# Stage 1 of a fused triangle layer: normalisation shifts stored as 16-byte pieces from tokens on partitions

## The chip, the core and the metric

The kernel runs on one core of a Trainium2 chip. Its five engines run their own instruction lists and meet at semaphores: TensorE (PE in the profile; PEld is its weight load), VectorE (DVE), ScalarE (ACT), GpSimd (POOL) and SyncE (SP), which here issues nearly all DMAs. The metric is device time in microseconds (us) for one execution, as the median of several. All data are float32.

## What is computed

Two layers over x of shape 384 x 384 x 128 (positions i and k, 128 channels). The first is a triangle layer, the second a gated row layer:

```
z     = layernorm(x)                                   # over the channels
left  = (z @ Wl + bl) * sigmoid(z @ Wlg + blg)
right = (z @ Wr + br) * sigmoid(z @ Wrg + brg)
core  = einsum('ikh,jkh->ijh', left, right)
x1    = x + sigmoid(x @ Wg + bg) * (layernorm(core) @ Wout + bout)

left2 = x1 @ W_left + b_left + x1 @ W_eq + b_eq
rsum  = sum over k of (x1 @ W_right + b_right)
y     = (left2 * rsum * sigmoid(x1 @ W_gate + b_gate)) @ W_out + b_out
out   = layernorm(y + x1)
```

The change is in the making of `left` and `right` alone.

## The kernel before

The kernel has three stages. Stage 1 makes `left` and `right` for all tokens and stores them to DRAM (`lr_d`). Stage 2 multiplies them channel by channel (L608). Stage 3 does everything that follows, row by row. Only stage 1 is touched.

Stage 1 works in 144 chunks. A chunk is 8 positions i times 128 positions k. It is done in two steps of four i each, so there are 288 steps. The code of a loop over `steps` is written out as one list for each engine, in program order. The order of the calls in that loop is the order of work on each queue.

The layer norm is split. Its weight is folded into the matrix `wz` (128 x 512), and its two numbers per token are used at different places:

- The scale `rs`, one over the standard deviation, is applied after the matmul, when PSUM is read out (L383 on ACT, L385 on DVE).
- The shift, a value per token that is subtracted from all channels, has to be applied to x before the matmul (L318 or L322 on GpSimd).

To get both, DVE runs `bn_stats` on tokens (L264, in `stats`), turns the results of a batch of chunks into means and variances (L276 to L280, in `powers`), GpSimd raises the variance to the power -1/2, one chunk at a time (L287, in `power`), and DVE makes the shift from it (L297 to L300, in `centres`). `LEAD` says how many steps the statistics run ahead of the steps that use them; `goal` gives their pace. Batches have one, two or four chunks.

The first 8 chunks are "plain". For them x lies with tokens on partitions, GpSimd subtracts the shift there (L318), and TensorE turns the result so that channels lie on partitions (L333). All other chunks load x a second time with channels on partitions (`columns`, L135). Their shift has to lie along the free dimension, in one row that is then broadcast over the partitions. `store_nd` does this: TensorE turns a batch's shifts (L348), ACT copies them out and halves them (L350), and SP stores them to the DRAM tensor `nd_d` (L351). Six steps before a step needs them, `load_shift` loads one row of 512 numbers (2 KB) back (L140). In `shift`, GpSimd broadcasts that row to all partitions (L321) and subtracts it from the columns (L322), two steps ahead of the matmuls.

In `back`, four matmuls with 512 output columns (L373) use 128 columns of x each as their weights.

GpSimd's instructions come from libraries that can be loaded. The loop asks for one twice (L470):

```
if k > 0:
    more = 4 if k in (6, len(steps) - 6) else 1
    while shifted < min(len(steps), k + 2 + more):
        shift(*steps[shifted])
        shifted += 1
    if more > 1:
        lib = library_config.all_libraries[10] if k == 6 else library_config.standard
        seq(nc.gpsimd.load_library(lib))
```

At step 6 it is the library with index 10, six steps before the end it is the standard one. In both places the subtractions of four steps are issued ahead of the load.

SP's queue is in order as well. It holds, for each step, a store of shifts if one is due, the columns of a chunk four ahead, one or more shift rows, a chunk of tokens, and a slice of `lr` (1 MB) to store. A DMA that has to wait holds back those behind it.

Of the kernel before, what the change touches and what calls it, by code (L numbers as in the profile page):

```python
# [8 lines left out]
F32 = mybir.dt.float32  # L9
AF = mybir.ActivationFunctionType  # L10
ALU = mybir.AluOpType
# [3 lines left out]
P = 128  # L15
# [4 lines left out]
def triangle_then_gated_row_kernel(ctx: ExitStack, tc: tile.TileContext, a: dict, out: bass.AP):  # L20
# [13 lines left out]
    nc = tc.nc  # L34
    x_nat, x_tok, x_row = a["x_nat"], a["x_tok"], a["x_row"]
    NG8, C = x_nat.shape[1], x_tok.shape[2]
    N = 8 * NG8
# [18 lines left out]
    def seq(ins):  # L56

        return tc.keep_in_program_order(ins)
# [21 lines left out]
    with ExitStack() as ctx2:  # L80
# [16 lines left out]
        with tc.tile_pool(name="p1w", bufs=5, side="right") as wp, \  # L97
# [1 line left out]
             tc.tile_pool(name="p1c", bufs=4, side="right") as xcp, \  # L99
             tc.tile_pool(name="p1n", bufs=4, side="right") as bcp, \  # L100
             tc.tile_pool(name="p1s", bufs=14, side="right") as sp, \
             tc.tile_pool(name="p1d", bufs=2, side="right") as dp, \
             tc.tile_pool(name="p1t", bufs=2, space=PSUM) as tps, \
             tc.tile_pool(name="p1p", bufs=3, space=PSUM) as pps:
            NQ = XR // 4
            AHEAD, LEAD = 4, 25
            TURN, FETCH = 9, 6
            HS = H // 8
            loaded, normed = {}, {}
            lr, full = {}, []  # L110
            batches, at = [(n, n + 1) for n in range(PLAIN)], PLAIN
            for size in [1, 1] + [2] * 7 + [4] * len(chunks):
                if at < len(chunks):
                    batches.append((at, min(at + size, len(chunks))))
                    at = batches[-1][1]
# [14 lines left out]
            def load_columns(n):  # L130

                if PLAIN <= n < len(chunks):
                    columns[n] = xcp.tile([P, XR, P], F32, tag="xt", name="xc")
                    src = x_tok[n // NG8, n % NG8]
                    seq(nc.sync.dma_start(out=columns[n].rearrange("c i k -> c (i k)"), in_=src))  # L135

            def load_shift(n, q):

# [84 lines left out]
            def late_weights():  # L223

                m2 = bcp.tile([P, 4 * P], F32, tag="bc", name="m2")[:, :C]
                seq(nc.vector.tensor_scalar(m2, avg, go, -0.5, ALU.mult, ALU.mult))

                seq(nc.vector.tensor_add(wleft, wleft, weq))
                seq(nc.vector.tensor_add(bleft, bleft, beq))

                seq(nc.vector.tensor_scalar(lns, lns, -1.0, None, ALU.mult))
                return m2
# [15 lines left out]
            def stats(n, q, half):  # L252

                if q == 0 and half == 0:
                    own = batch[n]
                    if n == own[0]:
                        g = XR * (own[1] - own[0])
                        terms[own] = [sp.tile([P, 4 * XR, 6], F32, tag="st", name="st", bufs=2)[:, :g]]
                    normed[n] = own, XR * (n - own[0])
                own, c0 = normed[n]  # L260
                st = terms[own][0][:, c0:c0 + XR]
                r0 = 4 * q + 2 * half
                for r in range(r0, r0 + 2):
                    seq(nc.vector.bn_stats(st[:, r, :], loaded[n][:, r, :]))  # L264

            def powers(own, lo, hi):

                if lo == 0:
                    g = XR * (own[1] - own[0])
                    terms[own] += [sp.tile(s, F32, tag=t, name=t, bufs=c)[:, :g] for t, s, c in  # L270
                                   ((f"mv{g}", [P, g, 2], {XR: 3, 2 * XR: 2}.get(g, 1)),
                                    ("nd", [P, 4 * XR], 3) if own[0] >= PLAIN else ("nd0", [P, XR], PLAIN),
                                    ("rs", [P, 4 * XR], 7) if own[0] >= PLAIN else ("rs0", [P, XR], PLAIN))]
                st, mv, sd, rs = (t[:, lo:hi] for t in terms[own])
                dv = st[:, :, 1]
                seq(nc.vector.tensor_add(mv, st[:, :, 1:3], st[:, :, 4:6]))  # L276
                seq(nc.vector.tensor_sub(dv, dv, st[:, :, 4]))
                seq(nc.vector.tensor_scalar(sd, mv[:, :, 1], 4.0 / C, 4.0 * EPS, ALU.mult, ALU.add))
                seq(nc.vector.tensor_mul(dv, dv, dv))
                seq(nc.vector.tensor_add(sd, sd, dv))  # L280
                pows.extend((own, c, min(c + XR, hi), (lo, hi)) for c in range(lo, hi, XR))

            def power():

                own, lo, hi, span = pows.pop(0)
                sd, rs = (t[:, lo:hi] for t in terms[own][2:])
                seq(nc.gpsimd.tensor_tensor(rs, sd, mhalf[:, :hi - lo], ALU.pow))  # L287
                if hi == span[1]:
                    means.append((own, span))

            def centres(count):

                for _ in range(count):
                    own, (lo, hi) = means.pop(0)
                    _, mv, nd, rs = (t[:, lo:hi] for t in terms[own])
                    nds[own] = terms[own][2]
                    seq(nc.vector.tensor_mul(nd, nd, rs))  # L297
                    seq(nc.vector.tensor_sub(nd, mv[:, :, 0], nd))
                    if own[0] < PLAIN:
                        seq(nc.vector.tensor_scalar(nd, nd, 0.5, None, ALU.mult))  # L300
                    centred[own] = now[0]

            centred, now = {}, [-1]

            def free(own):
                flying = {p[0] for p in pows} | {p[0] for p in means}
                size = own[1] - own[0]
                return sum(o[1] - o[0] == size for o in flying) < {1: 3, 2: 2}.get(size, 1)

            means = []  # L310

            def shift(n, q, rows=slice(0, 4)):


                s = slice(4 * q + rows.start, 4 * q + rows.stop)
                if n < PLAIN:
                    nd = nds[n, n + 1][:, s].unsqueeze(2).to_broadcast([P, rows.stop - rows.start, C])
                    seq(nc.gpsimd.tensor_tensor(loaded[n][:, s], loaded[n][:, s], nd, ALU.subtract))  # L318
                else:
                    z, t = columns[n][:, s].rearrange("c i k -> c (i k)"), shifts.pop((n, q))  # L320
                    seq(nc.gpsimd.partition_broadcast(t, t[0:1]))  # L321
                    seq(nc.gpsimd.tensor_tensor(z, z, t, ALU.subtract))  # L322

# [19 lines left out]

            def store_nd(own):

                g = XR * (own[1] - own[0])
                pt = tps.tile([P, 4, P], F32, tag="pt", name="pt")
                seq(nc.tensor.transpose(pt[:g, 0], nds.pop(own), ident))  # L348
                ndt = dp.tile([4 * XR, P], F32, tag="ndt", name="ndt", bufs=1)
                seq(nc.scalar.activation(ndt[:g], pt[:g, 0], AF.Copy, scale=0.5))  # L350
                seq(nc.sync.dma_start(  # L351
                    out=nd_d[own[0]:own[1]].rearrange("n (i k) -> (n i) k", k=P), in_=ndt[:g]
                ))

            def store_slice():
# [8 lines left out]
            def back(n, q, half, between=None):  # L364
# [5 lines left out]
                t = lr[kb, ig]  # L370
                pr = pps.tile([P, 2, 4 * H], F32, tag="pr", name="pr")
                for r in range(2):
                    seq(nc.tensor.matmul(  # L373
                        pr[:, r, :], lhsT=columns[n][:, 4 * q + 2 * half + r, :], rhs=wz, start=True, stop=True
                    ))
                    if r == 0 and between:
                        between()
# [56 lines left out]
                    power()  # L434
            shifted = 2
            waiting = batches[AHEAD // NQ:]
            turning = batches[PLAIN:]

            def goal(k):

                return 2 * (k + 1 + min(LEAD, 5 + min(k, 12 + (k - 12) // 3))) if k >= 0 else 2 * AHEAD

            for n in range(PLAIN, len(chunks)):
                k = 2 + (n - PLAIN) // 2
# [3 lines left out]

            def begin(k):

                while waiting and 2 * NQ * waiting[0][1] <= given and free(waiting[0]):
                    own = waiting.pop(0)
                    powers(own, 0, XR * (own[1] - own[0]))
                    if k > 0:
                        break

            for k, (n, q) in enumerate(steps):
                now[0] = k
                early = len(means)
                for _ in range(min(len(pows), 1)):  # L460
                    power()
# [28 lines left out]
                    power()  # L490
                if q == NQ - 1:
                    del loaded[n], normed[n], columns[n]
                while turning and turning[0] in centred and (
                        k >= centred[turning[0]] + 2 or NQ * turning[0][0] - 6 <= k):
                    store_nd(turning.pop(0))
                if q == NQ - 1:
                    load_columns(n + 4)
                for m, mq in steps[k + FETCH:k + FETCH + 1]:
                    if m >= PLAIN:
                        load_shift(m, mq)  # L500
                for m in fetch.get(k, []):
                    load_chunk(m)
                store_slice()
# [2 lines left out]
                        load(t, src)  # L506
                if k == 20:
                    m2 = late_weights()
                if k == 21:
                    late_products(m2)  # L510
                if k == len(steps) - 2 * G // 4 + 16:
                    assert not full
# [466 lines left out]
```

## Time and profile before

| | |
|---|---|
| median of 3 runs | 3164.53 us (3163.78 to 3166.14) |
| the profiled execution | 3163.46 us, span 3161.7 us |
| TensorE's clock | 0.999 of full |
| TensorE busy | 3141.8 us (99%) |
| DVE, GpSimd, ACT busy | 2454.2, 2396.7, 1811.4 us |
| last matmul of stage 1 (L373) ends | 1017.7 us |
| DMA queue of SP, share of 16 engines | 73.0% |

The span is the time from the first to the last instruction in the record. A group's row gives line, engine, operation, output and inputs with their shapes and the count; then the total busy time, the mean in ns of one, and the idle time of the engine just ahead of such instructions, with what ended it. In a timeline, a row begins with start and duration in us. In the chain of work that ended last, each piece is what the end of the kernel depended on at that moment.

### The profile page before, as it was taken

The page shows a single profiled execution, that of the slowest core. Times are in us where ns is not written, and L with a number is a line of the kernel's source. Part 1 is how long each engine was busy: PE and PEld are TensorE (multiplying, and loading weights), DVE is VectorE, ACT ScalarE, POOL GpSimd, SP SyncE. Part 2 cuts the span into 40 slices and gives each one's busy share as a digit, 9 for nine tenths or more (in the row PEclk, how much of TensorE's full clock was granted, in tenths as well). Part 3 has the DMA queues.
Part 4 walks back from the last instruction along what each step waited for, and adds up shares of the span by engine and source line. Part 5 has one row for each costly group of instructions (what it writes and reads, how often), then busy time and mean ns, then how long its engine had stood idle before and what let it go on. Part 6 is the DMA issues. An engine that isn't in the chain of part 4 may idle for free.

```text
span 3161.7 us, 44412 instructions
## 1 busy us (share of the span) xinstructions
PE 3141.8 (99%) x11345; PEld 1873.7 (59%) x11345; DVE 2454.2 (78%) x7208; ACT 1811.4 (57%) x3794; POOL 2396.7 (76%) x3045
## 2 busy tenths in 40 slices
PE   9999999999999999999999999999999999999998
PEld 4444444444444666666666666677777777777776
DVE  8888888788875555555555788888888888888998
ACT  4444444444444333343343577677777777777777
POOL 5888888888885666666666587788888888888887
PEclk9999999999999999999999999999999999999999
DMA  4887878788773999999999865666666666666562
GB/s 170 329 320 293 333 271 331 282 320 307 296 291 91 284 280 284 281 285 282 282 283 284 295 237 199 223 223 220 220 220 220 220 220 220 220 220 220 210 211 110
DMA packets 474845, 797.41 MB, mean 252 GB/s; under 512 B 21345, under 2 KB 385313, under 8 KB 458210
## 3 DMA queue, kind: packets, MB, share of 16 engines
q1 hardware_dynamic: 473296, 792.61, 73.0%
q8 instruction: 94, 1.54, 0.2%
q10 hardware_dynamic: 1234, 1.77, 0.2%
q14 instruction: 157, 1.29, 0.1%
q0 software_dynamic: 64, 0.20, 0.0%
HBM read 508.14 MB, written 286.36 MB: 251 GB/s over the span
## 4 chain that ended last, share of the span: by engine, by line
PE 97%; DVE 1%; POOL 1%; ACT 0%; issue 0%; DMA 0%; POOLq 0%; DVEq 0%; ACTq 0%
PE pr L373 30%; PE pc L608 23%; PE py L778 8%; PE pr L749 8%; PE pg L766 8%; PE pl L767 8%; PE pg L718 8%; PE py L779 4%; POOL rs L287 0%; DVE st L264 0%; DVE lr L385 0%; PE pq L726 0%; POOL stage L318 0%; PE pt L348 0%; PE pt L333 0%
## 5 line engine op out<-in xcount | busy, mean ns | idle before, releaser
L373 PE MATMUL pr<-wz,xc 128*128 128x512 f32 x2176 | 939.2, 592 | 0.0
L383 ACT ACTIVATE sg<-pr,rs 128x256 f32<-128x256 f32 x1152 | 482.9, 470 | 511.9 <-ACT sg L383 322.8
L608 PE MATMUL pc<-rr,lrh 128*128 128x384 f32 x2304 | 743.3, 486 | 0.4 <-DVE lr L385 0.4
L373 PEld LDWEIGHTS pr<-wz,xc 128*128 128x128 f32 x2176 | 408.0, 190 | 518.1 <-issue 440.9
L385 DVE SCALAR_TENSOR_TENSOR lr<-pr,rs,sg 128x256 f32<-128x256 f32 x1152 | 501.4, 476 | 195.1 <-ACT sg L383 194.5
L608 PEld LDWEIGHTS pc<-rr,lrh 128*128 128x128 f32 x2304 | 452.0, 196 | 291.9 <-issue 1.2
L813 ACT ACTIVATE py<-py,nm,rs 128x128 f32<-128x128 f32 x1149 | 492.1, 429 | 160.8 <-DVE u L771 79.0
L778 PEld LDWEIGHTS py<-wo,u 128*128 128x128 f32 x2304 | 376.6, 191 | 97.5
L619 DVE TENSOR_TENSOR csum<-csum,ct 128x1152 f32<-128x1152 f32 x127 | 176.6, 1391 | 329.0 <-ACT ct L617 329.0
L778 PE MATMUL py<-wo,u 128*128 128x128 f32 x2304 | 402.1, 275 | 0.0
L617 ACT COPY ct<-pc 128x1152 f32<-128x1152 f32 x127 | 142.2, 1119 | 445.2 <-PE pc L608 439.6
L740 POOL TENSOR_TENSOR cs<-ct,rt 128x384 f32<-128x384 f32 x380 | 379.6, 1000 | 7.6 <-PE pr L749 4.3
L848 POOL TENSOR_TENSOR yt<-yt,lnb 128x384 f32<-128x384 f32 x380 | 380.3, 1002 | 2.9 <-DVE yt L842 2.9
L322 POOL TENSOR_TENSOR xc<-xc,bc 128x512 f32<-128x512 f32 x272 | 345.4, 1270 | 24.0
L287 POOL TENSOR_TENSOR rs<-nd,mhalf 128x8 f32<-128x8 f32 (+1 forms) x145 | 236.2, 1629 | 153.0 <-DVE nd L280 145.5
L793 DVE BATCH_NORM_STATS2 st<-py 128x6 f32<-128x128 f32 x1152 | 266.0, 286 | 86.6 <-PE py L779 84.6
L779 PE MATMUL py<-ident,x1T 128*128 128x128 f32 x1152 | 314.0, 273 | 0.0
L749 PE MATMUL pr<-cs,wc 128*128 128x384 f32 x768 | 313.5, 490 | 0.0
L766 PE MATMUL pg<-x1T,mat_L_conv_W_gate 128*128 128x384 f32 x768 | 310.7, 486 | 0.9 <-ACT g L769 0.9
L718 PE MATMUL pg<-xt,mat_L_conv_Wg 128*128 128x384 f32 x768 | 310.7, 487 | 0.3 <-ACT ct L632 0.2
L767 PE MATMUL pl<-x1T,mat_L_conv_W_left 128*128 128x384 f32 x768 | 310.5, 486 | 0.0
L589 POOL COPY rr<-lrh 128x768 f32<-128x768 f32 x128 | 194.6, 1520 | 152.9 <-DMA lrh<-lr_d 141.9
(125 smaller groups left out, 4299.2 us busy)
## 6 DMA issues: line engine op xcount, KB each, us to landing
lr_d<-lr SPq DMA_DIRECT2D x128, 1024.0 KB
lrh<-lr_d SPq DMA_DIRECT2D x128, 640.0 KB
xt<-in_x_row_dram SPq DMA_DIRECT2D x96, 768.0 KB
ct<-core_d SPq DMA_DIRECT2D x95, 768.0 KB
rt<-rstd_d SPq DMA_DIRECT2D x95, 768.0 KB
out_dram<-yt SPq DMA_DIRECT2D x94, 768.0 KB
core_d<-ct SPq DMA_DIRECT2D x125, 576.0 KB
xt<-in_x_nat_dram SPq DMA_DIRECT2D x136, 512.0 KB
```

Source lines behind the costliest of these rows:

```text
L373: seq(nc.tensor.matmul(pr[:, r, :], lhsT=columns[n][:, 4 * q + 2 * half + r, :], rhs=wz, start=True, stop=True))
L383: seq(nc.scalar.activation(sg[r], pr[:, r, 2 * H:], AF.Sigmoid, scale=rs[r]))
L385: seq(nc.vector.scalar_tensor_tensor(t[:, :, c * XR + r0 + r, :], pr[:, r, :2 * H].rearrange("k (h s) -> k h s", s=2), rs[r], sg[r].rearra ...
L608: seq(nc.tensor.matmul(banks[ib], lhsT=t[:, kb, ib * P:(ib + 1) * P, 0], rhs=rr[:, kb], start=(kb == 0), stop=(kb == NB - 1),))
L718: seq(nc.tensor.matmul(pg[:, :N], lhsT=wg0, rhs=r["xT"], start=True, stop=True))
L749: seq(nc.tensor.matmul(pr[:, :N], lhsT=wc, rhs=r["cs"], start=True, stop=True))
L766: seq(nc.tensor.matmul(pg2[:, :N], lhsT=wgate, rhs=r["x1T"], start=True, stop=True))
L767: seq(nc.tensor.matmul(pl[:, :N], lhsT=wleft, rhs=r["x1T"], start=True, stop=True))
L778: seq(nc.tensor.matmul(py[:, s], lhsT=r["u"][:, s], rhs=r["wo"], start=True, stop=False))
L779: seq(nc.tensor.matmul(py[:, s], lhsT=r["x1T"][:, s], rhs=ident, start=False, stop=True, is_transpose=True))
L813: seq(nc.scalar.activation(py[:, s], py[:, s], AF.Identity, bias=bias, scale=scale))
L848: seq(engine.tensor_tensor(yt, yt, lnbb, ALU.add))
```

## The change

The shifts of the chunks that are not plain are no longer turned on TensorE. SP stores them from where they lie, with tokens on partitions: each partition holds, for each group of four i, four numbers in a row, and these 16 bytes go to DRAM as one piece. The row that is loaded back then has its numbers in the order (k, i) instead of (i, k). The host lays out x's columns (`x_tok`) in the same order, so a weight load for one i now takes every fourth number.

With it come these edits:

- Batches have two chunks at most; `LEAD` is 15 instead of 25, with another `goal`.
- `centres` takes two fused operations on DVE, which halve the shift as well. For plain chunks 1 to 7 it takes three operations on GpSimd, called directly behind the power.
- `store_nd` is called in the step in which the shift was made. A row is loaded six steps ahead, or later where its store is younger than two steps, and at the latest three steps ahead.
- `late_weights` gets a tile of its own, and `late_products` moves from step 21 to step 24.

The diff, cut to its core:

```diff
-            AHEAD, LEAD = 4, 25
-            TURN, FETCH = 9, 6
+            AHEAD, LEAD = 4, 15
+            FETCH = 6
...
-            for size in [1, 1] + [2] * 7 + [4] * len(chunks):
+            for size in [1, 1] + [2] * len(chunks):
...
-                    columns[n] = xcp.tile([P, XR, P], F32, tag="xt", name="xc")
+                    columns[n] = xcp.tile([P, NQ, P, 4], F32, tag="xt", name="xc")
...
-                m2 = bcp.tile([P, 4 * P], F32, tag="bc", name="m2")[:, :C]
+                m2 = wp.tile([P, C], F32, tag="m2", name="m2", bufs=1)
...
                 if hi == span[1]:
                     means.append((own, span))
+                    if 0 < own[0] < PLAIN:
+                        centres(1)
...
                     nds[own] = terms[own][2]
-                    seq(nc.vector.tensor_mul(nd, nd, rs))
-                    seq(nc.vector.tensor_sub(nd, mv[:, :, 0], nd))
-                    if own[0] < PLAIN:
-                        seq(nc.vector.tensor_scalar(nd, nd, 0.5, None, ALU.mult))
-                    centred[own] = now[0]
...
+                    if 0 < own[0] < PLAIN:
+                        seq(nc.gpsimd.tensor_tensor(nd, nd, rs, ALU.mult))
+                        seq(nc.gpsimd.tensor_tensor(nd, mv[:, :, 0], nd, ALU.subtract))
+                        seq(nc.gpsimd.tensor_scalar(nd, nd, 0.5, 0.0, ALU.mult, ALU.add))
+                    else:
+                        seq(nc.vector.scalar_tensor_tensor(nd, nd, 0.5, rs, ALU.mult, ALU.mult))
+                        seq(nc.vector.scalar_tensor_tensor(nd, mv[:, :, 0], 0.5, nd, ALU.mult, ALU.subtract))
+                    centred.append(own)
...
-                    z, t = columns[n][:, s].rearrange("c i k -> c (i k)"), shifts.pop((n, q))
+                    z, t = columns[n][:, q].rearrange("c k i -> c (k i)"), shifts.pop((n, q))
                     seq(nc.gpsimd.partition_broadcast(t, t[0:1]))
                     seq(nc.gpsimd.tensor_tensor(z, z, t, ALU.subtract))
...
             def store_nd(own):
-                g = XR * (own[1] - own[0])
-                pt = tps.tile([P, 4, P], F32, tag="pt", name="pt")
-                seq(nc.tensor.transpose(pt[:g, 0], nds.pop(own), ident))
-                ndt = dp.tile([4 * XR, P], F32, tag="ndt", name="ndt", bufs=1)
-                seq(nc.scalar.activation(ndt[:g], pt[:g, 0], AF.Copy, scale=0.5))
                 seq(nc.sync.dma_start(
-                    out=nd_d[own[0]:own[1]].rearrange("n (i k) -> (n i) k", k=P), in_=ndt[:g]
+                    out=nd_d[own[0]:own[1]].rearrange("n (q k i) -> k (n q) i", q=NQ, i=4),
+                    in_=nds.pop(own).rearrange("k (m i) -> k m i", i=4),
                 ))
...
-                        pr[:, r, :], lhsT=columns[n][:, 4 * q + 2 * half + r, :], rhs=wz, start=True, stop=True
+                        pr[:, r, :], lhsT=columns[n][:, 4 * q + i, :] if n < PLAIN else columns[n][:, q, :, i],
+                        rhs=wz, start=True, stop=True,
...
-                return 2 * (k + 1 + min(LEAD, 5 + min(k, 12 + (k - 12) // 3))) if k >= 0 else 2 * AHEAD
+                if k < 0:
+                    return 2 * AHEAD
+                return 2 * (k + 1) + min(2 * LEAD, 10 + (10 * k + 6) // 7 if k < 8 else 20 + 2 * (k - 7) // 3)
...
-                for m, mq in steps[k + FETCH:k + FETCH + 1]:
-                    if m >= PLAIN:
-                        load_shift(m, mq)
+                while want and want[0] <= k + FETCH and stored.get(want[0] // NQ, k) < k - (want[0] > k + 3):
+                    load_shift(*steps[want.pop(0)])
...
-                if k == 21:
+                if k == 24:
                     late_products(m2)
...
-    inputs["x_tok"] = blocks.transpose(2, 0, 4, 1, 3).reshape(N // P, N // 8, C, 8 * P)
+    blocks4 = x.reshape(N // 8, 2, 4, N // P, P, C)
+    inputs["x_tok"] = blocks4.transpose(3, 0, 5, 1, 4, 2).reshape(N // P, N // 8, C, 8 * P)
```

## The prediction

> **What bounds the kernel now.** I read the page first (busy times, slices, groups), then the windows of stage 1, then the chain that ended last, then GpSimd's own timeline, because the page says "PE 99%" and the question is who comes second.
>
> From the page:
>
> ```profile
> span 3161.7 us, 44412 instructions
> ...
> PE 3141.8 (99%) x11345; PEld 1873.7 (59%) x11345; DVE 2454.2 (78%) x7208; ACT 1811.4 (57%) x3794; POOL 2396.7 (76%) x3045
> ...
> L373 PE MATMUL pr<-wz,xc 128*128 128x512 f32 x2176 | 939.2, 592 | 0.0
> ...
> L322 POOL TENSOR_TENSOR xc<-xc,bc 128x512 f32<-128x512 f32 x272 | 345.4, 1270 | 24.0
> L287 POOL TENSOR_TENSOR rs<-nd,mhalf 128x8 f32<-128x8 f32 (+1 forms) x145 | 236.2, 1629 | 153.0 <-DVE nd L280 145.5
> ```
>
> TensorE is the bound and GpSimd has the least room behind it in stage 1. A hundred microseconds of stage 1 from the table by windows (busy us of PE, PEld, DVE, ACT, POOL, then clock, DMA share, GB/s), and the same stretch in the chain that ended last:
>
> ```profile
> 200.00:300.00 100.00, 100.00 (x237) 43.83 (x236) 80.85 (x255) 49.19 (x122) 83.41 (x74) 1.00 0.80 312
> ...
> 214.94 0.11 PE pt L348
> 215.05 27.48 PE pr L373 x64
> 242.53 0.11 PE pt L348
> ```
>
> TensorE has no gap there. Eight steps take 27.48 us plus 0.11 us for one turning (L348): 3.45 us a step. GpSimd in the same stretch (start, duration), in its order:
>
> ```profile
> 203.27 1.63 POOL L287 TENSOR_TENSOR rs<-nd,mhalf 128x8 f32<-128x8 f32 x1
> 204.89 0.80 POOL L321 PARTITION_BROADCAST bc<-bc  x1
> 205.78 1.27 POOL L322 TENSOR_TENSOR xc<-xc,bc 128x512 f32<-128x512 f32 x1
> ```
>
> A step needs one broadcast, 0.09 us to the next start, one subtraction and on average half a power: 0.80 + 0.09 + 1.27 + 0.82 = 2.98 us of 3.45. GpSimd's slack is 0.47 us a step; whatever adds more makes it the bound of all 272 steps that use columns.
>
> **What GpSimd's library loads cost now.** The kernel loads a GpSimd library at step 6 and another six steps before the end of stage 1 (L470). The instructions of that line, GpSimd's timeline around the first of them, and DVE's:
>
> ```profile
> L470 POOLq MODIFY_POOL_CONFIG  x4: 8/15/22, 43.9 to 1000.8; - x4
> ```
>
> ```profile
> 39.92 4.05 POOL L318 TENSOR_TENSOR stage<-stage,nd 128x512 f32<-128x512 f32 x4
> 49.27 3.31 POOL L287 TENSOR_TENSOR rs<-nd,mhalf 128x8 f32<-128x8 f32 x2 [5.30 <-DVE lr L385]
> ```
>
> ```profile
> 44.03 0.17 DVE L280 TENSOR_TENSOR nd<-nd,st 128x8 f32<-128x8 f32 x1
> ```
>
> GpSimd's timeline at the start of the kernel and at the end of stage 1:
>
> ```profile
> 1.23 0.28 POOL masks.py:199 TENSOR_SCALAR_AFFINE_SELECT ident<-ident 128x128 f32<-128x128 f32 x1 [0.30 <-POOL ident masks.py:197]
> ...
> 999.49 1.28 POOL L322 TENSOR_TENSOR xc<-xc,bc 128x512 f32<-128x512 f32 x1
> 1011.70 0.91 POOL L589 COPY rr<-lrh 128x768 f32<-128x768 f32 x1 [10.93 <-PE pr L373]
> ```
>
> The configuration instruction itself shows as nanoseconds. But after the four subtractions end at 43.97 the next power starts at 49.27, although its input (L280) was ready at 44.20. The releaser named, an L385, is no input of a power: the 5.30 us are the load. It is free now because four steps of subtractions are run ahead of it. The second load, at 1000.8, hides in a wait of 10.93 us for TensorE: it took at most that. At the very start a load of the library that is already there (masks.py:199) lets GpSimd go on after 0.30 us.
>
> [...] Weight loads of stage 2 step by 8 bytes and take 196 ns beside 190 for contiguous ones (L608, L373)[...]. [...]
>
> **The change, part by part.** Line numbers of the changed kernel are marked "new".
>
> 1. *Library switches.* The change moves the centring of plain chunks 1 to 7 to GpSimd, with a tensor_scalar as third operation (new L301). For chunks 6 and 7 that comes after the library load of step 6. In the instruction order that the changed source builds to, a bare library instruction stands ahead of that first tensor_scalar, and then one ahead of every broadcast (new L323, 272 of them) and one ahead of every subtraction (new L324, 272). The kernel before has none at these places. My reading: the library chosen at step 6 holds tensor_tensor and the broadcast, but not tensor_scalar; the builder puts the standard library back, which lacks the broadcast, and picks for the broadcast one that lacks tensor_tensor. From there the two alternate to the end of stage 1. Nothing brings step 6's library back. Cost: 544 x 5.30 = 2883 us, all on GpSimd, in order between broadcast and subtraction of the same chunk; the powers queue behind them. What hides it: 0.47 us a step of slack, so nothing does.
>
> 2. *GpSimd's sum.* From the first broadcast on: 272 x 0.796 = 216.5 broadcasts, 272 x 1.270 = 345.4 subtractions, 132 remaining powers x 1.63 = 215, loads 2883 (the 0.09 between broadcast and subtraction is inside the load's gap): 3660 us, or 13.5 a step. The first broadcast ran at 71.67 us before; I take 72, as the extra load at new L301 and 21 small centring operations (about 0.2 us each, from L797, L801 and L802: 201 to 204 ns) fall partly into waits of up to 5 us that GpSimd has there. GpSimd ends at 3732. TensorE then has one step left: 3.4 us[...]; I take 5. Stage 1 ends near 3737 instead of 1017.7 (the chain's last L373 stretch starts at 960.12 and lasts 57.59). That is 2719 us more.
>
> 3. *Turning removed.* 39 transposes on TensorE x 0.11 = 4.3 us and 39 copies of 0.25 us on ACT. On TensorE's pace worth 4.3; now hidden under GpSimd's 13.5 us: nothing. late_products moves from step 21 to 24 and gets its own tile; it removes a TensorE wait of 1.06 us, also nothing now.
>
> 4. *Batches of two, centring in two fused operations.* DVE, for four chunks: before 984 + 632 + 228 + 220 + 220 + 215 + 174 = 2673 ns. After, two batches of five operations at 16 wide (190 + 190 + 169 + 190 + 187 = 926) plus two fused ones, which no row shows: from 170 each[...] to 418[...]. That is 2532 to 3524 ns per 27.6 us: minus 0.1 to plus 0.9. DVE has 19 us of slack per 100. Hidden.
>
> 5. *16-byte pieces.* 69 stores instead of 39: 67 x 512 + 2 x 256 = 34,816 pieces, 2176 per DMA engine. No row has such a piece. From below nothing[...]. On SP 30 more issues of 0.32 us. A store is followed by its first shift load two steps later; SP would block there, and chunk loads, column loads and slice stores queue behind it. At 27 us for two steps there is no wait.
>
> 6. *Weight loads at a 16-byte step.* From 190 ns to four times that, 760: then 8 x 0.76 = 6.1 us a step, under 13.5. Hidden. The broadcast row and x's columns have the same order, so the subtraction stays contiguous and keeps its 1.27 us.
>
> 7. *Lead of 15 instead of 25.* Statistics begin ten steps later relative to use; from statistics to use there are still about twelve steps. No cost at this pace.
>
> Sum against the profiled execution's own time, 3163.5 (span 3161.7): 3163.5 + 2719 = 5882. The median of the three runs is 1 us above that execution, so I say 5885.
>
> **Rivals.**
>
> *Switches are nearly free (ends faster).* If two libraries once loaded stay in memory and a switch is only a pointer, as the 0.30 us at masks.py:199 could be read, stage 1 remains TensorE's. It decides at 0.47 us for both switches of a step. Then 3164.5 - 4.3 - 1.1 = 3159, provided pieces cost under 83 ns each (180 us idle per engine over 2176) and weight loads under 430 ns, TensorE's pace per pass. Against it: 5.30 us at the only real change of library that can be timed.
>
> *The standard library takes longer.* The one load of it is bounded only by 10.93 us. With 10.9 for it and 5.3 for the other: 5.6 x 272 = 1523 more, 7408 us.
>
> *One of the two is cheap.* If putting the standard library back costs only the 0.3 us: 5.0 x 272 = 1360 less, 4525 us. For it: that load has never been seen to cost anything. Against: nothing in the trace separates them.
>
> *Store and load of shifts as the bound.* Worth something only under the first rival; counted there.
>
> **How the numbers follow.** Forecast 0.80 (two full loads a step), nearly free 0.06, long standard library 0.08, one cheap 0.06. In the forecast each microsecond of both loads together is 272 us: 7.35 us a pair gives 5000, 15.1 gives 7100. [...] I take 5000 to 7100, longer upward since two of the libraries are untimed; it holds most of the forecast and the milder part of the long-library case, and leaves out the rest: 2 in 10. A measurement of this kernel can tell about 0.2%, 6 us. The nearly free case (about 3159) is mostly faster by 0.2% or on the line: faster 0.05, same 0.01, slower 0.94.
>
> **What would show it.** Right: TensorE busy near 3.5 of every 13.5 us in stage 1, waiting on the subtraction; GpSimd idle some 5 us before each broadcast and each subtraction, with over a thousand library instructions in its queue; stages 2 and 3 as long as before. Wrong: broadcast and subtraction back to back at 0.09 us, and stage 1 ending near 1015; or gaps before broadcast and subtraction that differ widely, which would be the second or third rival.

## The result: 6779.83 us, 2.14 times the time before

The changed kernel takes 6779.83 us (median, 6772.53 to 6786.53) beside 3164.69 us for the kernel before (3163.78 to 3166.14): a ratio of 2.142, 95% interval 2.140 to 2.144. The prediction was 5885 us, with 5000 to 7100 as its range.

The page of the changed kernel, with the rows that answer to those shown of before (line numbers are those of the changed kernel from here on; 372 was 373, 324 was 322, 323 was 321):

```profile
span 6774.9 us, 45606 instructions
...
PE 3834.8 (57%) x11306; PEld 2147.0 (32%) x11306; DVE 2453.8 (36%) x7395; ACT 1805.9 (27%) x3755; POOL 2399.3 (35%) x3066
...
L372 PE MATMUL pr<-wz,xc 128*128 128x512 f32 x2176 | 1631.4, 917 | 2917.6 <-POOL xc L324 2917.6
...
L324 POOL TENSOR_TENSOR xc<-xc,bc 128x512 f32<-128x512 f32 x272 | 340.5, 1252 | 1947.3 <-issue 1947.3
L323 POOL PARTITION_BROADCAST bc<-bc x272 | 218.7, 804 | 1822.4 <-issue 1815.8
```

Read the last two rows first. GpSimd's work has not grown: the broadcasts take 218.7 us and the subtractions 340.5, beside 216.4 and 345.4 before. What is new is the idle time ahead of them, 1822.4 and 1947.3 us, put down to "issue": GpSimd waits for nothing that the profile shows. The matmuls then wait 2917.6 us for the subtraction. No engine is busy for more than 57% of the span, so the busy shares alone name no bound.

GpSimd's timeline in the middle of stage 1 (start, duration; in brackets the idle time ahead), and the instructions of the two lines in its queue:

```profile
2005.39 1.25 POOL L324 TENSOR_TENSOR xc<-xc,bc 128x512 f32<-128x512 f32 x1 [6.91 <-issue]
2014.34 0.80 POOL L323 PARTITION_BROADCAST bc<-bc  x1 [7.70 <-issue]
2022.35 1.25 POOL L324 TENSOR_TENSOR xc<-xc,bc 128x512 f32<-128x512 f32 x1 [7.22 <-issue]
2023.58 1.68 POOL L286 TENSOR_TENSOR rs<-nd,mhalf 128x8 f32<-128x8 f32 x1
2031.20 0.80 POOL L323 PARTITION_BROADCAST bc<-bc  x1 [5.94 <-issue]
```

```profile
L323 POOLq MODIFY_POOL_CONFIG  x544: 1/1/11, 77.2 to 4611.3; - x182
...
L324 POOLq MODIFY_POOL_CONFIG  x544: 129/129/129, 84.6 to 4617.8; - x182
```

The power (L286) starts without a gap behind the subtraction; both are tensor_tensor operations. In this stretch only a change between subtraction or power and broadcast costs time. Each of the two lines has 544 configuration instructions for 272 steps: two for each switch, and they take 1 and 129 ns (medians). The microseconds lie behind them and belong to no instruction.

TensorE in a thousand microseconds of stage 1 (busy us and count of PE, PEld, DVE, ACT, POOL; granted clock; DMA share; GB/s), and the chain that ended last, where stage 1 ends:

```profile
2000.00:3000.00 1000.00, 355.95 (x475) 149.38 (x476) 165.31 (x574) 98.89 (x236) 172.17 (x149) 0.64 0.18 64
```

```profile
4617.91 6.87 issue
4624.78 1.26 POOL xc L324
4626.09 6.01 PE pr L372 x8
4632.10 68.17 PE pc L611 x211
```

TensorE is busy a third of the time, and the clock that it was granted is 0.64 of full on average: a matmul takes 917 ns on average instead of 592. The same place in the chain of the kernel before:

```profile
960.12 57.59 PE pr L373 x135
...
1018.86 1.21 PE pc L608 x3
```

Stage 2 begins at 4632.10 us instead of 1018.86, which is 3613.2 us later. The span grew by 6774.9 - 3161.7 = 3613.2. So all of the loss is in stage 1, and stages 2 and 3 take 2142.8 us in both kernels. (The 1017.7 us in the table of before is where the chain leaves stage 1; the last matmul of that stage starts at 1017.9 and ends at 1018.5.)

### The profile page after: what moved, and what is told of

Read it like the earlier page. It is cut to its first block, busy times and chain, and to the rows that moved or that the text cites. A ratio compares the mean times of both kernels' runs of the same rounds, so it can differ in the third digit from the quotient of the medians.

```text
span 6774.9 us, 45606 instructions
## 1 busy us (share of the span) xinstructions
PE 3834.8 (57%) x11306; PEld 2147.0 (32%) x11306; DVE 2453.8 (36%) x7395; ACT 1805.9 (27%) x3755; POOL 2399.3 (35%) x3066
## 5 line engine op out<-in xcount | busy, mean ns | idle before, releaser
L372 PE MATMUL pr<-wz,xc 128*128 128x512 f32 x2176 | 1631.4, 917 | 2917.6 <-POOL xc L324 2917.6
L372 PEld LDWEIGHTS pr<-wz,xc 128*128 128x128 f32 x2176 | 683.4, 326 | 3865.0 <-POOL xc L324 3127.8
L324 POOL TENSOR_TENSOR xc<-xc,bc 128x512 f32<-128x512 f32 x272 | 340.5, 1252 | 1947.3 <-issue 1947.3
L323 POOL PARTITION_BROADCAST bc<-bc x272 | 218.7, 804 | 1822.4 <-issue 1815.8
L801 POOL TENSOR_TENSOR rs<-rs,mhalf 128x6 f32<-128x6 f32 x192 | 256.2, 1334 | 16.0
```

What stands on the lines that cost most here:

```text
L372: seq(nc.tensor.matmul(pr[:, r, :], lhsT=columns[n][:, 4 * q + i, :] if n < PLAIN else columns[n][:, q, :, i], rhs=wz, start=True, stop=Tr ...
```

## Experiments

**1. The tensor_scalar alone is replaced.** Centring of plain chunks stays on GpSimd, at the same place and with three operations, but all three are tensor_tensor: (shift - mean) x (-0.5) with the constant tile that the power uses. All else of the change is kept.

```diff
-                        seq(nc.gpsimd.tensor_tensor(nd, mv[:, :, 0], nd, ALU.subtract))
-                        seq(nc.gpsimd.tensor_scalar(nd, nd, 0.5, 0.0, ALU.mult, ALU.add))
+                        seq(nc.gpsimd.tensor_tensor(nd, nd, mv[:, :, 0], ALU.subtract))
+                        seq(nc.gpsimd.tensor_tensor(nd, nd, mhalf[:, :hi - lo], ALU.mult))
```

> The changed kernel, with the third operation of the centring on GpSimd written as a tensor_tensor (nd*rs minus the mean, times the row of -0.5 that the powers use) in place of the tensor_scalar; nothing else. Theory (library switches are the whole loss): no bare library instruction is left at the broadcasts and subtractions, stage 1 is TensorE's again, about 3159 us (3153 to 3166). Rival (16-byte pieces, weight loads at a 16-byte step or the shorter lead are part of the loss): stage 1 stays longer than before, 3200 us or more.

Measured: 3162.11 us, ratio to before 0.9991 (0.9983 to 0.9999). The library instructions ahead of broadcasts and subtractions are gone from the built order, and 3618 us with them. From its page, the matmuls, the weight loads and the subtractions:

```profile
L372 PE MATMUL pr<-wz,xc 128*128 128x512 f32 x2176 | 938.2, 594 | 3.8 <-POOL xc L324 3.8
L372 PEld LDWEIGHTS pr<-wz,xc 128*128 128x128 f32 x2176 | 670.5, 308 | 270.8 <-POOL xc L324 5.9
L324 POOL TENSOR_TENSOR xc<-xc,bc 128x512 f32<-128x512 f32 x272 | 345.9, 1272 | 24.0
```

The gap ahead of the subtraction is back at 24.0 us for 272, or 0.09 each. One instruction's kind decides, not where the centring is done. It also leaves one wait of 3.8 us for a subtraction, to which experiments 7 to 9 return.

**2. Plain centring on VectorE**, with the two fused operations that the other chunks use.

```diff
-                    if 0 < own[0] < PLAIN:
-                        seq(nc.gpsimd.tensor_tensor(nd, nd, rs, ALU.mult))
...
-                    else:
-                        seq(nc.vector.scalar_tensor_tensor(nd, nd, 0.5, rs, ALU.mult, ALU.mult))
-                        seq(nc.vector.scalar_tensor_tensor(nd, mv[:, :, 0], 0.5, nd, ALU.mult, ALU.subtract))
+                    seq(nc.vector.scalar_tensor_tensor(nd, nd, 0.5, rs, ALU.mult, ALU.mult))
+                    seq(nc.vector.scalar_tensor_tensor(nd, mv[:, :, 0], 0.5, nd, ALU.mult, ALU.subtract))
```

> The changed kernel, with the centring of plain chunks on DVE (the two fused operations that the other chunks have), called at the same place. Theory: again no switches, about 3159 us plus what DVE loses by waiting for seven powers in order (up to 2 us each, while TensorE runs ahead): 3158 to 3175. Rival: as for the first, 3200 or more.

Measured: 3170.89 us, ratio 1.0019 (1.0011 to 1.0027). No switches here either. It is slower than experiment 1 by 8.8 us, and the waits of TensorE that are new lie in the first 116 us: 3.6 us at 52 us for VectorE's statistics, and 2.9 and 2.0 us, ending at 99 and 115 us, for subtractions on columns.

**3. The kernel before, with one tensor_scalar on GpSimd** at step 8, two steps after the library of step 6 is loaded. It works on a 128 x 1 scratch tile that no result needs.

```diff
+                if k == 8:
+                    seq(nc.gpsimd.tensor_scalar(warm, warm, 0.5, 0.0, ALU.mult, ALU.add))
```

> The kernel before, with one tensor_scalar on GpSimd of 128x1 at step 8, on a tile of no further use. Theory: this one instruction brings the 544 switches back and with them about 6780 us, without any other part of the change. Rival (the change's other parts carry a good part of the loss): clearly under 6500.

Measured: 6742.08 us, in a single execution. From this kernel's rows by form, between 100 and 4500 us (its lines 321 and 322 are broadcast and subtraction):

```profile
L322 POOL TENSOR_TENSOR xc<-xc,bc 128x512 f32<-128x512 f32 x264 | 330.5, 1252 | 1870.5 <-issue 1870.5
L321 POOL PARTITION_BROADCAST bc<-bc x264 | 212.6, 805 | 1764.4 <-issue 1757.1 <-DMA xc<-in_x_tok_dram 7.3
```

Gaps of 7.09 and 6.68 us. The kernel before with one added instruction, which has almost no work to do, shows the effect but for 38 us, of which gaps shorter by 0.07 and 0.04 us make up some 29. Storing by pieces, batches, lead and the order of columns have no larger part in it.

**4. The changed kernel with step 6's library loaded once more**, directly behind the centring of the last plain chunk.

```diff
                         centres(1)
+                        if own[0] == PLAIN - 1:
+                            seq(nc.gpsimd.load_library(library_config.all_libraries[10]))
```

> The changed kernel with one more load of the library of index 10, right behind the last plain centring. Theory: two switches are left at steps 6 and 7 (one at the first tensor_scalar after the load, one here), 6 to 7 us each, of which the subtractions run ahead hide part: 3162 to 3180 us. Rival: 3200 or more.

Measured: 3175.02 us, ratio 1.0035 (1.0022 to 1.0048). The tensor_scalar stays, but it costs two switches and not 544: GpSimd idles 8.56 us ahead of it and 5.14 us behind the load put in. They aren't hidden at this place: TensorE waits 11.3 us at once for a plain subtraction (L322 of that kernel). Its waits for a subtraction on columns, 3.8 us in two, aren't switches: the longer one, 3.5 us at 104 us, stands behind a broadcast that waited 4.97 us for its row, as in experiment 1. This shows that it is the state which the tensor_scalar leaves behind that costs, since nothing brings step 6's library back.

**5. Another library for the subtraction.** The changed kernel, with the library of index 1 asked for ahead of each broadcast and that of index 10 ahead of each subtraction, instead of the standard one.

```diff
                     z, t = columns[n][:, q].rearrange("c k i -> c (k i)"), shifts.pop((n, q))
+                    seq(nc.gpsimd.load_library(library_config.all_libraries[1]))
                     seq(nc.gpsimd.partition_broadcast(t, t[0:1]))
+                    seq(nc.gpsimd.load_library(library_config.all_libraries[10]))
                     seq(nc.gpsimd.tensor_tensor(z, z, t, ALU.subtract))
```

> The changed kernel, with both switches of a shift written out, and the subtraction under the library of index 10 in place of the standard one (the broadcast's library is the same as in the changed kernel). It asks why a switch costs 6.7 and 7.2 us here and 5.30 in the kernel before. If each library has its own price: the gap before the subtraction is about 5.3 us, total near 6270. If the traffic of stage 1 is what lengthens a switch: gap about 7 us, total near 6740.

Measured: 6118.72 us in a single execution, 661 less than the changed kernel. Rows by form between 100 and 4500 us, where 326 is the subtraction and 324 the broadcast, and then those of the changed kernel:

```profile
L326 POOL TENSOR_TENSOR xc<-xc,bc 128x512 f32<-128x512 f32 x271 | 339.6, 1253 | 1331.7 <-issue 1331.7
L324 POOL PARTITION_BROADCAST bc<-bc x271 | 218.7, 807 | 1762.4 <-issue 1743.5 <-DMA xc<-in_x_tok_dram 13.2 <-DMA lr_d<-lr 5.7
```

```profile
L324 POOL TENSOR_TENSOR xc<-xc,bc 128x512 f32<-128x512 f32 x262 | 328.0, 1252 | 1874.4 <-issue 1874.4
L323 POOL PARTITION_BROADCAST bc<-bc x263 | 211.4, 804 | 1767.6 <-issue 1761.1 <-DMA xc<-in_x_tok_dram 6.6
```

The gap ahead of the subtraction is 4.91 us instead of 7.15 in the same stretch of the changed kernel, and ahead of the broadcast it is 6.50 instead of 6.72. 272 x (2.24 + 0.22) = 669 us, close to the difference. So a load has a price that depends on the library, and that of index 10 is the cheapest of the three: 4.91 here, 5.30 once in the kernel before.

**6. More traffic.** The changed kernel with each 1 MB slice of `lr` stored twice, to ask whether a load is longer because it shares the DMA with other transfers.

```diff
-                    seq(nc.sync.dma_start(
+                    for _ in range(2):
+                        seq(nc.sync.dma_start(
...
```

> The changed kernel, with every 1 MB slice of lr stored twice (the same bytes to the same place). If traffic lengthens the switches: the gaps grow, before the broadcast from 6.70 to about 7.2 us, in all 150 us or more on 6780. If it does not: 6780 within 20 us.

Measured: 6862.9 us in a single execution, 83 more than the changed kernel. Neither expectation was met. The rows of the same stretch:

```profile
L324 POOL TENSOR_TENSOR xc<-xc,bc 128x512 f32<-128x512 f32 x257 | 321.7, 1252 | 1944.0 <-issue 1944.0
L323 POOL PARTITION_BROADCAST bc<-bc x257 | 206.6, 804 | 1709.8 <-issue 1696.5 <-DMA lr_d<-lr 13.3
```

The gap ahead of the subtraction grew from 7.15 to 7.56 us (1944.0 / 257), that ahead of the broadcast went from 6.72 to 6.65 (1709.8 / 257). So with twice the stores one of the two loads was longer by 0.41 us and the other was not. That is too little to make the difference between 7 us and 5.

**7. The early wait of experiment 1.** In that kernel the chain that ended last leaves TensorE between 70 and 100 us. Its pieces around the wait:

```profile
82.12 1.60 POOL rs L286
83.72 5.21 issue
...
88.98 0.81 POOL bc L323
...
89.87 1.27 POOL xc L324
...
91.18 8.88 PE pr L372 x14
```

The 5.21 us are a row of shifts that isn't there: its store was issued at 77.5 us and SP could issue the load only at 84.3, when the store had landed (SP waits 2.7 us for it there); the broadcast followed at 88.98. TensorE then needs 8.88 us for 14 passes that take 6.0 at full clock (27.48 us for 64). The edit lets the statistics, and so the store, run ahead faster in the first steps:

```diff
-                return 2 * (k + 1) + min(2 * LEAD, 10 + (10 * k + 6) // 7 if k < 8 else 20 + 2 * (k - 7) // 3)
+                return 2 * (k + 1) + min(2 * LEAD, 10 + 2 * k if k < 8 else 24 + 2 * (k - 7) // 3)
```

> Kernel: the multiply version (no tensor_scalar on GpSimd), and statistics pulled ahead faster at the start: the lead grows by two half steps a step for k below 8 (10 + 2k, then 24 + 2(k-7)/3) instead of 10/7. Theory: the one early wait of 3.8 us of the multiply version (TensorE for the subtraction at 84 to 91 us) comes from the store of the third pair's shifts, issued at 77.5, and its rows, issued at 84.3 to 85.1 and landing at 88.9. Statistics two steps earlier put the store some 7 us earlier: the wait falls under 1 us, stage 1 ends near 1012, time 3158.5 (3156.5 to 3161). Rival: VectorE has no room this early and the extra statistics delay other work: 3162 to 3167.

Measured: 3154.97 us, ratio 0.9971 (0.9960 to 0.9983), the best of all kernels here and below the expected 3156.5 to 3161. The matmuls of its page, and where its stage 1 ends in the chain:

```profile
L372 PE MATMUL pr<-wz,xc 128*128 128x512 f32 x2176 | 934.4, 592 | 0.0
```

```profile
939.61 69.17 PE pr L372 x162
1008.79 0.03 issue
```

The chain leaves stage 1 at 1008.79 us, beside 1015.60 in experiment 1. The 6.8 us are 3.8 of waiting and 2.9 of slow passes behind the wait; the expectation had left out the second. TensorE's windows from 80 to 100 us show it, for experiment 1 and then for this kernel:

```profile
80.00:100.00 20.00, 16.20 (x33) 9.66 (x32) 12.20 (x47) 6.58 (x16) 13.90 (x13) 0.83 1.04 374
```

```profile
80.00:100.00 20.00, 20.00 (x48) 14.38 (x47) 17.86 (x67) 9.76 (x24) 16.02 (x15) 1.00 1.03 393
```

**8. Smaller batches instead.** Experiment 1 with four batches of a single chunk at the start of the columns instead of two.

```diff
-            for size in [1, 1] + [2] * len(chunks):
+            for size in [1, 1, 1, 1] + [2] * len(chunks):
```

> Kernel: the multiply version, with the first four batches behind the plain chunks of one chunk instead of the first two. Theory: the shifts of chunk 10 no longer wait for the statistics of chunk 11, so its store leaves about 3 to 4 us earlier and the wait of 3.8 us falls to under 1: 3158.5 (3156.5 to 3161). Rival: the wait moves on to the next batch, or is set by the flight of store and load behind the 1 MB slices and not by when the store is issued: 3161 to 3164.

Measured: 3162.08 us, ratio 0.9993 (0.9985 to 1.0002). The rival's case. The wait moved to the next batch and grew: 6.0 us between 100 and 120 us, where a store issued at 87.99 was followed by its load at 97.35 and the broadcast at 104.92. It is the flight of store and load that has to be given time, 9.4 us from store to load and 7.6 from load to broadcast; a smaller batch doesn't shorten it. From 80 to 100 us this kernel's DMA share is 1.03; what makes the flight so long, no run shows.

**9. The early pace with plain centring on VectorE**: experiment 2's edit and experiment 7's together.

> Kernel: plain centring on VectorE (no GpSimd centring, no switch) together with the early pace of the statistics that took the early wait away in the multiply version (3154.97 there). Theory: without that wait, where the plain chunks are centred still matters at the start, since VectorE is busy 18 to 20 us of every 20 in the first 60 us; the first matmul on columns comes as late as with VectorE's centring before (81.9 without the early pace, 74.3 with GpSimd's centring), so 3160 to 3167. Rival: the difference of 8.8 us between the two placings was the early wait's alone: 3154 to 3158.

Measured: 3164.49 us, ratio 0.9999 (0.9991 to 1.0008), as the theory had it. With the starts of the first and last matmul on columns (L373, L372 and L367 in their kernels), in us, the three sum up as follows:

| kernel | first | last | between |
|---|---|---|---|
| before | 77.1 | 1017.9 | 940.8 |
| 7, centring on GpSimd | 74.3 | 1009.0 | 934.7 |
| 9, centring on VectorE | 84.3 | 1018.9 | 934.6 |

So the change, without its switches and with the early pace, gains 6.1 us in the stretch on columns, whoever centres the plain chunks; there the turnings and the wait of late_products are gone. Placing the centring is worth another 10 us ahead of that stretch (9.5 in the medians). In the kernel of experiment 9 TensorE waits 3.2 us at once, released by VectorE's statistics (L275), and its next eight passes take 6.60 us where the eight behind them take 3.60; its mean clock from 40 to 60 us is 0.83. Those are 6.2 us; the rest isn't taken apart.

## Why the prediction was right, and where it was off

**Step 1, the switches: right in mechanism and count, too small in size.** There are 544 of them and each stands ahead of a broadcast or a subtraction. One tensor_scalar causes them (experiments 1 and 3), and it is the missing return of step 6's library that makes them last (4). The term that was mis-sized is the price of a switch. I took 5.30 us for each, the only load that the kernel before allowed me to time, and it was a load of the library of index 10. The two that alternate are others. The gaps are 6.70 us (1822.4 / 272) and 7.16 us (1947.3 / 272), together 13.86 instead of 10.60: 272 x 3.26 = 887 us of the 895 by which 5885 was short. Experiment 5 shows that the price goes with the library. What about a library makes it dear, its size or something else, no run shows.

**Step 2, GpSimd's sum: right in form.** 218.7 + 340.5 + 1822.4 + 1947.3, and 132 powers of 1.65 us, give 4547 us. From the first broadcast's gap at 77.0 us that ends at 4624; the last subtraction ended at 4626. That gap began at 77.0 us and not at 72, because the switch ahead of the tensor_scalar (8.31 us) was not absorbed by waits as far as I had assumed. TensorE's last step took 6.01 us where I took 5, an estimate above its 3.4 us in the kernel before. My sign "TensorE busy near 3.5 of every 13.5 us" was off too: it is busy 36% of a step of 16.7 us, about 6 us, as it was granted less clock (0.64 from 2000 to 3000 us, where the kernel before has 1.00 in its stage 1, for example from 200 to 300 us). That stays hidden behind GpSimd.

**Step 3, the turning: hidden, as said.** The whole change without the switches is worth 6.1 us in the stretch on columns, where I had 4.3 for the turnings and 1.1 for the wait of late_products; no run has either of the two alone.

**Step 4, VectorE's batches: hidden in every kernel.** In experiment 1 it is busy 83.47 us of the 100 from 200 on, where the kernel before had 80.85: plus 0.72 us in 27.6, inside my -0.1 to +0.9. One of the two fused operations (L304) was outside its bracket of 170 to 418 ns, though, my estimate from rows of the kernel before (418 is its L297 at 16 wide, four of them from 100 to 1000 us):

```profile
L304 DVE SCALAR_TENSOR_TENSOR nd<-mv,nd 128x16 f32<-128x16 f32 x65 | 37.1, 570 | 2.2
L303 DVE SCALAR_TENSOR_TENSOR nd<-nd,rs 128x16 f32<-128x16 f32 x65 | 20.9, 321 | 0.0
```

In the changed kernel, from 100 to 4500 us, the same two take 175 and 165 ns. GpSimd is busy 172 us of the 1000 from 2000 on there, and 83.47 us of the 100 from 200 on in experiment 1; whether that makes the difference, no run shows.

**Step 5, the 16-byte pieces: hidden, and near to nothing.** From 100 to 1000 us, SP's DMA queue in experiment 1 and in the kernel before (packets, MB, share of 16 engines):

```profile
q1 hardware_dynamic: 93027, 264.39, 79.7%
```

```profile
q1 hardware_dynamic: 60149, 264.22, 77.5%
```

32,878 more packets are 2055 per DMA engine. They took 2.2% of 900 us, 19.8 us: 9.6 ns each, where the first rival could bear 83. That is a rough estimate: over the whole execution the shares are 73.3% of 3160.3 us and 73.0% of 3161.7, 8.5 us apart on each engine, or 4 ns for each of 34,224 more packets on 16 engines. The way through DRAM is not new, since the kernel before stores and loads its shifts too. SP holds back a load until the store has landed (in experiment 1, 107.8 us in 31 waits from 100 to 1000 us, 4.3 at most); with the new pace that becomes the wait of experiments 1 and 8, which belongs to step 7.

**Step 6, weight loads at a 16-byte step: hidden.** 308 ns beside 190, 1.6 times the time, of a bracket from 190 to 760 whose upper end was my estimate, four times the 190. Eight of them are 2.46 us in a step of 3.44.

**Step 7, the lead: no cost in the changed kernel, as said.** Without the switches the pace that the change gives the statistics in the first steps costs 6.8 us, which the forecast had no need to see and the first rival (3159) left out.

**The rivals.** Nearly free switches: excluded by 13.86 us a step. The 0.30 us on which that rival rests are seen again where a library is asked for that is already there. At the end of stage 1 the changed kernel loads the standard library (its L471, at 4626.3 us), which the last subtraction has left in place:

```profile
4624.78 1.25 POOL L324 TENSOR_TENSOR xc<-xc,bc 128x512 f32<-128x512 f32 x1 [6.95 <-issue]
4626.34 0.86 POOL L592 COPY rr<-lrh 128x768 f32<-128x768 f32 x1 [0.30 <-issue]
```

A long standard library: true in kind, as it is the dearer of the two, at 7.16 instead of 10.9 us. One cheap: false; the load of the standard library that I could only bound was the longest. A load that hides in a wait of 10.93 us says nothing of its length.

## What to carry to other kernels

Where GpSimd runs operations from loadable libraries, look through its built instruction order for library instructions inside the loop before looking at any duration: one operation that is outside the loaded library, once, can leave it in a state in which every step switches twice, here 13.86 us a step and 3613 us in all. Stay with operations that the loaded library has (a multiplication by a constant tile in place of a tensor_scalar, 3162.11 us in experiment 1), or load the wanted library again behind the exception (3175.02 us in experiment 4). And a handover through DRAM wants its lead counted from the landing of the store and not in steps, at the moment when it takes longest: here 9.4 us from store to load and 7.6 from load to broadcast (experiment 8).

## What was unexpected of the hardware

- The three libraries have different prices: 4.91 us (index 10; gaps of 4.75 to 5.30 where it was loaded once), 6.50 to 6.72 us (index 1), 7.09 to 7.16 us (the standard one). Doubling the stores of `lr` changed the last two by -0.07 and +0.41 us.
- A wait of 3.8 us was followed by half of TensorE's clock. In windows of 1 us of experiment 1 the granted clock is 1.00 up to 89 us and again from 97, and 0.50 from 90 to 96; only the two windows in which it changes lie between (0.80 and 0.79). The 0.64 of the changed kernel is a mean over such stretches: in its 34 windows of 1 us from 2000 to 2034 us the clock is 1.00 or 0.50, with five between (0.57 to 0.74). In experiment 1 the clock fell some 2.2 us after TensorE's last pass and rose again some 5 us after its work had resumed. So behind a single wait of 3.8 us, passes of up to 1243 ns instead of 592 cost another 2.9 us. The length of a wait alone doesn't decide: in experiment 2 waits of 1.47 and 0.46 us, ending at 21.2 and 22.3 us, were followed by 3.4 us at 0.50, and in experiment 9 the same two waits were not.
- A 16-byte store piece took 4 to 10 ns of a DMA engine's time, by the estimates of step 5, when it ran among transfers of 512 KB and 1 MB.
